# A fused transformer block: a new order of the first weight loads, and matmuls of zeros ahead of the first product

## The chip, the cores and the metric

The kernel runs on one core of a Trainium2 chip. The core has a matrix engine (TensorE, in the profile PE, with its weight loads as PEld), a vector engine (VectorE, DVE), a scalar engine (ScalarE, ACT), a general engine (GpSimd, POOL) and a queue engine (SyncE, SP) that here only issues DMA transfers. The metric is the device time of one execution in microseconds, as the median of several executions; lower is better.

## The reference

The input `x` has 32 sequences of 64 tokens with 1024 features, in float32. The block computes

```
x = x + attention(cond(x, label))
x = x + ffn(cond2(x, language))
```

- `cond(x)` is `x @ W.T` plus a low-rank term whose A factor is picked per sequence by its label (rank 32, 5 labels).
- `attention` projects the result to queries, keys and values (`qkv = c @ w_qkv.T + b_qkv`, 32 heads of 32, 8 key/value heads), applies a rotary embedding, does causal softmax attention within each sequence, and projects back with `w_o`.
- `cond2(x)` is `x @ W.T` plus a mixture of 8 experts of rank 16, the two best of a router with a language bias; `ffn` is the same form with a base matrix, a bias and another router.

Between `cond` and the projection to q, k and v there is no nonlinearity. So the two weight matrices can be multiplied with each other once, and the product applied to the tokens. The same holds for `cond2` and `ffn`.

## The kernel before, in words

All matrices are kept with the contracted dimension on the 128 partitions; 1024 features are 8 chunks of 128 (`KC = 8`, `H = KC // 2 = 4`).

**The stages.** First the kernel multiplies weight matrices: `cq` (the conditioning matrix by the query part of `w_qkv`, 1024 columns), `ckv` (by the key and value part, 512 columns) and `cf` (the second conditioning matrix by the ffn's). The products go to scratch memory in HBM. Then, for each half of the tokens, come the products `qk`, `v`, the attention, `o` and the ffn `f`.

**How one product is done.** A product runs in four groups. A group covers 256 output rows (two blocks of 128), all 8 contracted chunks and two halves of 512 columns. With the two halves of each dimension it is a 2x2 by 2x2 block product, done with seven block products instead of eight (Strassen's method in Winograd's form). Each block product is four matmuls, one per chunk of a half (`mult`, L247 to L259), with 128x512 operands. POOL forms the sums of weight blocks (`weight_sums`, L163 to L174, four operations a group), DVE forms the sums of column blocks (`column_sums`, L176 to L188). In the class `Group` the steps are named p1 to p7:

- `p1` uses the first half of the weights' chunks, left output block (`w[:, :h, :P]`), and chunks 0 to 3 of the columns, left half.
- `p2` uses the second half of the weights' chunks and chunks 4 to 7 of the columns, left half, and adds to p1's bank.
- `p6`, `p5`, `p7` and `p4` use the sums of columns t2, t1, t3 and t4; `p6`, `p5`, `p7` and `p3` use the sums of weights.

**The first product, around which the change lies** (L561 to L638). `wq` holds the columns: 8 chunks of 1024 columns, 512 KB each. `w0` and `w1` are the weights of groups 0 and 1, 1 MB each; the first half of their chunks (`first_half`, 0 to 3) and the second half are loaded apart. `b1` is the other factor of the low-rank term. All these loads are issued by SP, in the written order. The loads before are, in this order: w0's first half, left outputs (256 KB); chunk 0 of wq, left half (256 KB); w0's first half, right outputs; chunk 0, right half; b1 (128 KB); chunks 1, 2, 3 whole (512 KB each); w1's first half; w0's second half; chunks 4 to 7; w1's second half; then `index` and the constants.

**The order on the engines.** Up to L697 SP, TensorE and DVE run in the written order (`manual_schedule`). ACT and POOL are ordered by a planner that estimates when each operation's inputs are ready; behind L697 it orders all engines, except where the code writes an order out again. Loads use eight completion counters in turn, so SP issues a load only when the one eight places before it has landed. TensorE's written order at the start is: p1 of group 0; the first half of `b1q_rows` (b1 by chunks 0 to 3 of wq, both column halves, left first; 16 records of 32 output columns); p1 of group 1; p2 of group 0; the second half of `b1q_rows` (chunks 4 to 7); p2 of group 1; p6 of group 0; and so on (L624, L625, and the dictionary `after`). DVE forms t1 (chunk by chunk, from chunks 0 to 3, right minus left), then t2 (which needs chunks 4 to 7, right halves), then t3; t4 comes after p6 of group 0, with `labels_and_languages`, which needs `index` and the constants.

**Temporaries.** `tmp` (L95) takes one of 11 buffers of 128x512 in SBUF, `ps_tile` (L89) one of 5 banks of PSUM.

Of the kernel before, what the change touches and what calls it, by code (L numbers as in the profile page):

```python
# [19 lines left out]
P = 128  # L20
D = 1024
KC = D // P
# [54 lines left out]
def block_kernel(ctx: ExitStack, tc: tile.TileContext, a, out: bass.AP):  # L77
    nc = tc.nc
# [10 lines left out]
    def ps_tile(name):  # L89
        return psum.tile([P, 512], F32, tag="ps", name=name)  # L90
# [4 lines left out]
    def tmp(name):  # L95
        return tp.tile([P, 512], F32, tag="t", name=name)
# [15 lines left out]
    def load_x(hf):  # L112
# [10 lines left out]
            engines={mybir.EngineType.SP, mybir.EngineType.PE, mybir.EngineType.DVE}  # L123
        )
    )
    bqk, bo, bb = biases[:, 0:10], biases[:, 10 : 10 + KC], biases[:, 10 + KC :]

    lab = const.tile([P, B], F32, tag="lab", name="lab")
# [29 lines left out]
    H = KC // 2  # L158
# [314 lines left out]
    with tc.tile_pool(name="gen", bufs=1) as gen:  # L473
# [87 lines left out]
        wq = gen.tile([P, KC, D], F32, tag="right", name="wq")  # L561
# [3 lines left out]
        b1 = gen.tile([P, KC, LR], F32, tag="b1", name="b1")  # L565
        w0, w1 = (wp.tile([P, KC, WG], F32, tag="w", name=f"w_cq{g}") for g in range(2))
        first_half, second_half = slice(0, H), slice(H, KC)

        for r in range(2):
            cols, outs = slice(r * D // 2, (r + 1) * D // 2), slice(r * P, (r + 1) * P)  # L570
            nc.sync.dma_start(w0[:, first_half, outs], a["w1"][0, :, first_half, outs])
            nc.sync.dma_start(wq[:, 0, cols], a["wqkv"][:, 0, cols])
        nc.sync.dma_start(b1, a["b1"])
        for half in (first_half, second_half):
            for kc in range(max(half.start, 1), half.stop):
                nc.sync.dma_start(wq[:, kc, :], a["wqkv"][:, kc, :D])
            nc.sync.dma_start(w1[:, half], a["w1"][1, :, half])
            if half is first_half:
                nc.sync.dma_start(w0[:, second_half], a["w1"][0, :, second_half])
        nc.sync.dma_start(index, a["index"])  # L580
        nc.sync.dma_start(cst, a["consts"])
        b1q_rows = rank_rows("b1q", b1, wq, D, b1q)
# [188 lines left out]
    for hf in range(2):  # L771
# [396 lines left out]
        for c in range(2):  # L1168
            rows = ps_tile(f"lgrows_{hf}_{c}")
            for kc in range(KC):  # L1170
# [5 lines left out]
                    start=(kc < 4),  # L1176
                    stop=(kc >= 4),
# [3 lines left out]
            for i in range(4):  # L1181
# [5 lines left out]
                    start=True,  # L1187
                    stop=True,
# [63 lines left out]
        ps = ps_tile(f"lgx_{hf}")  # L1252
        for t in range(NT):
# [4 lines left out]
                start=True,  # L1258
                stop=True,
            )  # L1260
        gates3 = gates_of("3", hf, ps[:, : NT * E].rearrange("p (t e) -> p t e", e=E), lg3)
        for c in range(2):
            ps = ps_tile(f"hx_{hf}_{c}")
# [98 lines left out]
```

## Time and profile before

| | |
|---|---|
| time, median of 3 runs | 1222.43 us (1219.89 to 1223.11) |
| the profiled execution's own time | 1215.41 us |
| its span, first to last instruction | 1213.6 us |
| PE busy | 1200.8 us |
| DVE busy | 577.8 us |
| POOL busy | 511.1 us |
| ACT busy | 153.7 us |
| read from HBM, written to it | 83.72 MB, 24.22 MB |

A line of the timeline gives the start in microseconds from the span's start, the length, the engine, the line of the code, the operation, the output and the inputs by name, the shapes and the number of records merged; in brackets stands how long the engine was idle before it and what ended that. A float32 matmul leaves two records. In the list of waits the numbers behind the colon are the total in microseconds, how often, and the longest. In the table of windows each row is a stretch of time, with the busy time of each engine, the clock, the busy share of the DMA engines and the GB/s that they moved.

### The profile page before, as it was taken

Reading aid. Unit: us, or ns where it says so; the run is one execution under the profiler, and the core shown is the slowest. Engines: PE = TensorE matmul, PEld = TensorE weight load, DVE = VectorE, ACT = ScalarE, POOL = GpSimd, SP = SyncE. Lnnn points to the kernel's source line nnn. Section 1 sums busy time; section 2 is a strip of 40 time slices with the busy share of each in tenths; the row PEclk is TensorE's granted clock in tenths of the full one; section 3 lists DMA queues with packets and bytes.
Section 4 is the critical chain, followed back from the end, with each engine's and each line's share of the span. In section 5 each row is a group of like instructions: output and inputs, shape, how many; then the busy total and the mean of one; then the engine's idle time right before and its main releaser. Section 6 shows DMA issues by size and latency. Waiting matters only on the chain.

```text
span 1213.6 us, 13600 instructions
## 1 busy us (share of the span) xinstructions
PE 1200.8 (99%) x5434; PEld 611.3 (50%) x5434; DVE 577.8 (48%) x940; ACT 153.7 (13%) x282; POOL 511.1 (42%) x437
## 2 busy tenths in 40 slices
PE   7999999999999999999999999999999999999998
PEld 2444874555444477544444444444468544444443
DVE  4313151114457789753942113456789764842111
ACT  1000100000001124330000000100214330000000
POOL 4441351442533746754726011542756653821010
PEclk9999999999999999999999999999999999999999
DMA  6562741645111122023114225111120123112110
GB/s 240 186 236 86 263 161 55 205 163 166 35 35 35 36 70 70 12 75 126 36 35 139 69 96 182 36 35 35 35 71 21 51 70 113 63 35 69 56 50 35
DMA packets 58560, 108.83 MB, mean 90 GB/s; under 512 B 5120, under 2 KB 35200, under 8 KB 57216
## 3 DMA queue, kind: packets, MB, share of 16 engines
q1 hardware_dynamic: 42704, 79.53, 19.6%
q10 hardware_dynamic: 13104, 20.03, 4.5%
q0 software_dynamic: 2688, 8.39, 2.1%
q8 instruction: 43, 0.70, 0.2%
q14 instruction: 21, 0.17, 0.0%
HBM read 83.72 MB, written 24.22 MB: 89 GB/s over the span
## 4 chain that ended last, share of the span: by engine, by line
PE 99%; DMA 0%; SPq 0%; DVE 0%; issue 0%; DVEq 0%
PE qk_y L249 9%; PE o_y L249 7%; PE f_y L249 7%; PE qk_x L249 6%; PE qk_z L249 6%; PE v L864 5%; PE f_z L249 5%; PE o_x L249 5%; PE o_z L249 5%; PE f_x L249 5%; PE cq_y L249 3%; PE cf_y L249 3%; PE sc L885 3%; PE cq_x L249 2%; PE pt L938 2%; PE cf_z L249 2%
## 5 line engine op out<-in xcount | busy, mean ns | idle before, releaser
L814 POOL TENSOR_TENSOR raw<-raw,consts 128x512 f32<-128x512 f32 x40 | 63.1, 1586 | 105.8 <-DVE t L813 105.8
L918 POOL TENSOR_TENSOR e<-e,top 128x512 f32<-128x512 f32 x64 | 65.0, 1044 | 57.3 <-DVE top L917 42.2
L930 POOL TENSOR_TENSOR e<-e,tot 128x512 f32<-128x512 f32 x64 | 66.2, 1066 | 27.3 <-DVE tot L928 27.3
L249 PE MATMUL qk_y<-sum_x,s_qk 128*128 128x512 f32 x160 | 72.2, 594 | 0.0
L249 PE MATMUL qk_x<-x,w_qk 128*128 128x512 f32 x160 | 72.2, 594 | 0.0
L170 POOL TENSOR_TENSOR s_f<-w_f 128x512 f32<-128x512 f32 x8 | 11.5, 1437 | 121.2 <-DMA w_f<-cffn 97.4
L249 PE MATMUL o_x<-q,w_o 128*128 128x512 f32 x128 | 58.9, 592 | 0.0
L864 PE MATMUL v<-w_v,x 128*128 128x256 f32 x256 | 58.7, 382 | 0.0
L249 PE MATMUL f_x<-x,w_f 128*128 128x512 f32 x128 | 57.9, 592 | 0.0
L249 PE MATMUL f_y<-sum_y,s_f 128*128 128x512 f32 x128 | 57.5, 592 | 0.0
L1039 POOL TENSOR_TENSOR x<-x,o_u 128x512 f32<-128x512 f32 x24 | 30.9, 1291 | 54.3 <-DVE o_u L1037 33.2
L864 PEld LDWEIGHTS v<-w_v,x 128*128 128x128 f32 x256 | 47.4, 190 | 8.4 <-issue 2.7
L249 PEld LDWEIGHTS qk_x<-x,w_qk 128*128 128x128 f32 x160 | 30.1, 190 | 38.0 <-issue 37.9
L815 DVE TENSOR_TENSOR t<-t,consts 128x512 f32<-128x512 f32 x40 | 48.8, 1231 | 0.7
L249 PEld LDWEIGHTS qk_y<-sum_x,s_qk 128*128 128x128 f32 x160 | 30.2, 190 | 37.1 <-issue 36.6
L170 POOL TENSOR_TENSOR s_qk<-w_qk 128x512 f32<-128x512 f32 x10 | 19.2, 1923 | 65.9 <-DMA w_qk<-cqkv 65.8
L927 DVE TENSOR_REDUCE tot<-e 128x8 f32<-128x512 f32 x64 | 40.5, 667 | 10.7 <-ACT e L922 10.4
L922 ACT ACTIVATE e<-e 128x512 f32<-128x512 f32 x64 | 38.3, 641 | 54.3 <-POOL e L918 54.2
L908 DVE TENSOR_TENSOR e<-sc,consts 128x512 f32<-128x512 f32 x64 | 39.7, 677 | 8.8 <-PE sc L885 8.8
L249 PEld LDWEIGHTS f_x<-x,w_f 128*128 128x128 f32 x128 | 24.3, 190 | 30.6 <-issue 30.6
L249 PEld LDWEIGHTS f_y<-sum_y,s_f 128*128 128x128 f32 x128 | 24.3, 190 | 30.6 <-issue 30.6
L917 DVE TENSOR_REDUCE top<-e 128x8 f32<-128x512 f32 x64 | 39.6, 676 | 0.0
(318 smaller groups left out, 2202.4 us busy)
## 6 DMA issues: line engine op xcount, KB each, us to landing
w_qk<-cqkv SPq DMA_DIRECT2D x10, 1024.0 KB, 6.2
x<-in_xT SPq DMA_DIRECT2D x16, 512.0 KB, 7.7
w_o<-in_wo SPq DMA_DIRECT2D x16, 512.0 KB, 5.2
s_o<-wos SPq DMA_DIRECT2D x16, 512.0 KB, 6.3
w_f<-cffn SPq DMA_DIRECT2D x8, 1024.0 KB, 5.3
outT<-o ACTq DMA_DIRECT2D x32, 256.0 KB, 2.5
cqkv<-cq ACTq DMA_DIRECT2D x16, 256.0 KB, 2.2
w_ckv<-in_w SPq DMA_DIRECT2D x4, 1024.0 KB, 7.2
```

What stands on the lines that cost most here:

```text
L249: nc.tensor.matmul(ps, self.weights[left][:, kc, :], self.right(right, kc), start=first and kc == 0, stop=kc == self.h - 1, skip_group_che ...
L814: nc.gpsimd.tensor_mul(rv, rv, c3)
L815: nc.vector.tensor_mul(t2v, t2v, s3)
L864: nc.tensor.matmul(begun[t], x[kc][:, t * P : (t + 1) * P], wv[:, kc, :], start=False, stop=kc == KC - 1, skip_group_check=True,)
L885: nc.tensor.matmul(sc[j][:, n * S : (n + 1) * S], q[rows, g, b, 2 * mp : 2 * mp + 2, :].rearrange("p m t -> p (m t)"), k[rows, g, b, :], s ...
L908: nc.vector.tensor_add(per_key(e), per_key(sc[j]), mask.unsqueeze(1).to_broadcast([P, 8, S]))
L917: nc.vector.tensor_reduce(top, ev, AX.X, ALU.max)
L918: nc.gpsimd.tensor_sub(ev, ev, wide(top))
L922: nc.scalar.activation(e, e, AF.Exp, scale=SCALE)
L927: nc.vector.tensor_reduce(tot[:, i], es[i], AX.X, ALU.add)
L930: nc.gpsimd.tensor_mul(es[i], es[i], wide(tot[:, i]))
L1039: nc.gpsimd.tensor_add(xo, xo, to)
```

## The change

Two things change. At the start of the written order, DVE sets a temporary of 128x512 to zero, and TensorE multiplies this temporary by itself three times, with 512, 512 and 128 columns, into a bank of PSUM that nobody reads.

The order and cut of the first loads is another. The new order is: w0's first half, left outputs; the left halves of chunks 0 to 3 of wq (four loads of 256 KB); b1; the right halves of chunks 0 to 3; w1's first half; w0's first half, right outputs; w0's second half; chunks 4 to 7; w1's second half. The bytes are the same; three loads more are issued (18 before `index` instead of 15). The order of TensorE's and DVE's other work is as it was.

```diff
@@ -123,6 +123,12 @@
             engines={mybir.EngineType.SP, mybir.EngineType.PE, mybir.EngineType.DVE}
         )
     )
+
+    idle = tmp("idle")
+    nc.vector.memset(idle, 0.0)
+    ps = ps_tile("idle")
+    for n in (512, 512, 128):
+        nc.tensor.matmul(ps[:, :n], idle[:, :P], idle[:, :n], start=True, stop=True)
     bqk, bo, bb = biases[:, 0:10], biases[:, 10 : 10 + KC], biases[:, 10 + KC :]
@@ -566,17 +572,20 @@
         w0, w1 = (wp.tile([P, KC, WG], F32, tag="w", name=f"w_cq{g}") for g in range(2))
         first_half, second_half = slice(0, H), slice(H, KC)
 
-        for r in range(2):
-            cols, outs = slice(r * D // 2, (r + 1) * D // 2), slice(r * P, (r + 1) * P)
-            nc.sync.dma_start(w0[:, first_half, outs], a["w1"][0, :, first_half, outs])
-            nc.sync.dma_start(wq[:, 0, cols], a["wqkv"][:, 0, cols])
-        nc.sync.dma_start(b1, a["b1"])
-        for half in (first_half, second_half):
-            for kc in range(max(half.start, 1), half.stop):
-                nc.sync.dma_start(wq[:, kc, :], a["wqkv"][:, kc, :D])
-            nc.sync.dma_start(w1[:, half], a["w1"][1, :, half])
-            if half is first_half:
-                nc.sync.dma_start(w0[:, second_half], a["w1"][0, :, second_half])
+        outs = [slice(r * P, (r + 1) * P) for r in range(2)]
+        nc.sync.dma_start(w0[:, first_half, outs[0]], a["w1"][0, :, first_half, outs[0]])
+        for c in range(2):
+            cols = slice(c * D // 2, (c + 1) * D // 2)
+            for kc in range(H):
+                nc.sync.dma_start(wq[:, kc, cols], a["wqkv"][:, kc, cols])
+            if c == 0:
+                nc.sync.dma_start(b1, a["b1"])
+        nc.sync.dma_start(w1[:, first_half], a["w1"][1, :, first_half])
+        nc.sync.dma_start(w0[:, first_half, outs[1]], a["w1"][0, :, first_half, outs[1]])
+        nc.sync.dma_start(w0[:, second_half], a["w1"][0, :, second_half])
+        for kc in range(H, KC):
+            nc.sync.dma_start(wq[:, kc, :], a["wqkv"][:, kc, :D])
+        nc.sync.dma_start(w1[:, second_half], a["w1"][1, :, second_half])
         nc.sync.dma_start(index, a["index"])
         nc.sync.dma_start(cst, a["consts"])
         b1q_rows = rank_rows("b1q", b1, wq, D, b1q)
```

## The prediction

> **What bounds the kernel now.** The page comes first: one engine is busy for the whole span, so time can only be won where that engine stands or crawls.
>
> ```profile
> span 1213.6 us, 13600 instructions
> PE 1200.8 (99%) x5434; PEld 611.3 (50%) x5434; DVE 577.8 (48%) x940; ACT 153.7 (13%) x282; POOL 511.1 (42%) x437
> ```
>
> TensorE lacks 12.8 us of the span. The waits of TensorE say where:
>
> ```profile
> PE cq_x L249 <- DMA wq<-in_wqkv: 7.1, 2, 4.7
> PE cq_y L249 <- DVE cq_u L291: 0.8, 1, 0.8
> PE f_z L249 <- issue: 0.6, 1, 0.6
> ```
>
> 7.1 us of it wait for the first weights, in the stretch that the change rewrites; all other waits together are under 2 us. The timeline of TensorE shows the head (start, length, what, records; a 512-column float32 matmul leaves two records):
>
> ```profile
> 4.67 2.05 PE L249 MATMUL cq_x<-wq,w_cq 128*128 128x512 f32 x2 [4.67 <-DMA wq<-in_wqkv]
> 9.15 4.78 PE L249 MATMUL cq_x<-wq,w_cq 128*128 128x512 f32 x6 [2.44 <-DMA wq<-in_wqkv]
> 13.87 1.92 PE L503 MATMUL b1q<-wq,b 128*32 128x512 f32 x16
> 15.72 7.13 PE L249 MATMUL cq_x<-wq,w_cq 128*128 128x512 f32 x16
> 22.78 1.92 PE L503 MATMUL b1q<-wq,b 128*32 128x512 f32 x16
> 24.64 3.70 PE L249 MATMUL cq_x<-wq,w_cq 128*128 128x512 f32 x8
> 28.18 3.60 PE L249 MATMUL cq_y<-sum_cq,s_cq 128*128 128x512 f32 x8
> ```
>
> In program order these are step p1 of group 0 (chunks kc 0 to 3, left halves), the first half of the b1q rows, p1 of group 1 together with p2 of group 0 (chunks 4 to 7), the second half of b1q, p2 of group 1, p6 of group 0. From 13.87 on nothing stands; before it, p1 of group 0 takes from 4.67 to 13.9. Two causes: chunk 1 is there only at 9.15, and the matmuls are slow. The weight loads show the second:
>
> ```profile
> 11.87 0.33 PEld L249 LDWEIGHTS cq_x<-wq,w_cq 128*128 128x128 f32 x1 [0.52 <-DMA wq<-in_wqkv]
> 12.73 0.33 PEld L249 LDWEIGHTS cq_x<-wq,w_cq 128*128 128x128 f32 x1 [0.52 <-issue]
> 17.11 0.19 PEld L249 LDWEIGHTS cq_x<-wq,w_cq 128*128 128x128 f32 x1 [0.24 <-issue]
> 17.54 0.19 PEld L249 LDWEIGHTS cq_x<-wq,w_cq 128*128 128x128 f32 x1 [0.24 <-issue]
> ```
>
> One record each 0.86 us at 12 us, each 0.43 us at 17 us: TensorE runs at half speed until about 13 us. (The clock column reads 1.00 there too; the spacing is the better witness.) Last, when loads land, by who stopped waiting for them:
>
> ```profile
> 6.73 1.15 DVE L182 TENSOR_TENSOR sum_cq<-wq 128x512 f32<-128x512 f32 x1 [6.73 <-DMA wq<-in_wqkv]
> 9.13 0.69 DVE L182 TENSOR_TENSOR sum_cq<-wq 128x512 f32<-128x512 f32 x1 [1.25 <-DMA wq<-in_wqkv]
> 14.33 1.28 POOL L170 TENSOR_TENSOR s_cq<-w_cq 128x512 f32<-128x512 f32 x1 [6.99 <-DMA w_cq<-in_w]
> 15.64 5.70 DVE L184 TENSOR_TENSOR sum_cq<-wq,sum_cq 128x512 f32<-128x512 f32 x4 [3.23 <-DMA wq<-in_wqkv]
> 20.76 1.70 POOL L170 TENSOR_TENSOR s_cq<-w_cq 128x512 f32<-128x512 f32 x1 [0.57 <-DMA w_cq<-in_w]
> ```
>
> Chunk 0 is whole at 6.73, chunk 1 at 9.13 (chunks 2 and 3 at 10.43 and 11.72, by the next two DVE rows), w0's second half at 14.33, chunk 4 at 15.64, w1's second half at 20.76. From 9.13 a 512 KB load lands each 1.28 to 1.30 us, so chunk 7 landed at about 15.64 + 3 x 1.28 = 19.5. The windows say that this stream is full:
>
> ```profile
> 5.00:9.00 4.00, 1.72 (x2) 0.14 (x1) 1.15 (x1) 0.00 (x0) 1.26 (x1) 1.00 0.98 315
> 16.00:20.00 4.00, 4.00 (x10) 1.73 (x10) 4.00 (x3) 0.54 (x1) 3.92 (x3) 1.00 1.03 406
> ```
>
> (The last two columns: DMA share, GB/s.) The DMA engines have no idle time from 5 to 20 us. So there are two bounds in a row: p1 holds TensorE back until 13.9, while the stream, in the same bytes, lets p2 of group 0 end no earlier than chunk 7's landing plus one chunk's two records, 19.5 + 0.86 = 20.4. It ended at 22.78. The gap of 2.4 us is what a faster p1 can win at most with this stream.
>
> **The change part by part.**
>
> *Zeros.* A DVE memset of 128x512 and matmuls of 512, 512 and 128 columns. No DVE memset is in the trace: 0.10 us (POOL's 128x1 memsets) to 1.15 us (the longest L182); I take 0.69, the usual L182 of that size. Engines start at 0.75, so the zeros start at about 1.5. At the slow spacing they are 0.99 (4.67 to 5.66, the first pair) + 3 x 0.86 + 2 x 0.21 for the short one = 4.0 us, to 5.5 (4.9 to 6.0 by the memset's ends). Behind them queues p1, which started at 4.67: 0.8 us later. In exchange it can run at 0.43 a record: before, the spacing fell about 4 us after TensorE resumed at 9.15, and the zeros run for 4. p1 then ends at 5.5 + 8 x 0.43 = 8.9; if zeros do not count for the clock, 4 us after 5.5 it does: 5.5 + 4.0 (4.7 records) + 3.3 x 0.43 = 10.9. Both ends are covered by the next wait.
>
> *Order of loads.* Ahead of p1's last chunk now lie 256 KB of w0 and four pieces of 256 KB (1.3 MB) instead of 2.75 MB. The 1.05 MB ahead of chunk 0's right half landed at 6.73, so 1.3 MB lands at about 7.7 even at the 278 GB/s below, in time for p1's chunk 3 at 5.5 + 6 x 0.43 = 8.1.
>
> *Price of the smaller pieces.* Rows of 2 KB instead of 4 KB for chunks 1 to 3. By the packet records a 2 KB packet took about 87 ns and a 4 KB one 160: eight packets per DMA engine and piece, 2 x 8 x 87 = 1.39 us a chunk against 1.28, so 0.33 us for three chunks. Ends: 0 (nothing lost) and 0.65, if all 1.57 MB move at the 278 GB/s of the first 1.18 MB (to about 6.0) and not in the 5.0 us from 6.73 to 11.72. I take 0.33, which is the same packet at the same place. SP issues three loads more, 0.43 to 0.50 us each; it is ahead of the stream by up to eight loads, so they are hidden. Without that cover: 1.5 us on the stream.
>
> *What the stream gives then.* w0's right outputs (512 packets of 512 B, 32 per engine at 28 ns = 0.9 us) go behind w1's first half. Chunk 3's right half: 11.72 - 0.9 + 0.33 = 11.15. w1's first half was one 1.30 us step after chunk 3, 13.0; now 13.0 - 0.9 + 0.33 = 12.4. From w0's second half on, the bytes ahead are the same: chunk 4 at 15.97, chunk 7 at 19.8, w1's second half at 21.1.
>
> *TensorE then.* b1q's first half waits for the right halves and ends at about 12. p1 of group 1: 12.4 to 15.85. p2 of group 0 is fed by chunks at 15.97, 17.25, 18.5, 19.8: ends 19.8 + 0.86 = 20.7 against 22.78. Then 1.85 of b1q to 22.5 (w1 there since 21.1), p2 of group 1 to 26.0, p6 at 26.0 instead of 28.18. **Gain 2.1 us** (1.75 with 0.65, 2.4 with 0).
>
> *What else moves.* p6 at 26.0 needs DVE's t2 and POOL's second sum. DVE's t2 began at 15.64 and took 5.70; 0.33 later it ends at 21.7. DVE's next four take 5.71, to 27.4, before p6's result at 29.5. POOL's L172 of group 0 ran at 6.08; its input now lands near 13.3. Its reader p7 comes at about 34.5, and POOL's eight sums, 1.27 to 1.72 each, fit between. The second sum ended at 18.5. If that cover were gone, p6 would wait and everything behind it. index and consts go behind three more issues and land near 22, while the consts are first read at 31.6 (29.5 now) and index at 34.9 (32.8). The zeros' bank and temporary are free long before their next use. Later loads wait for TensorE's releases (47.30 and on), so they move with it. The 2.1 us therefore stays to the end, unless the order of the rest changes.
>
> *Sum.* The profiled execution was 1215.41 (span 1213.6 plus 1.8 outside); 1213.3 after. It lay 7.0 under the median of the runs, 1222.43, to which I apply the same difference: **1220.3**.
>
> **Two rules against the rows.** The row: half speed up to 12.73, full at 15.7, in one execution. The Trainium skill (TensorE: Matmul & The Clock Gate, Part 1) says that the clock is halved until a free-running window of about 3.4 us has been busy. By that, an estimate, other executions of before get full speed anywhere from 12.6 to 16.0, b1q would be slow in some, and the gain would be 2.1 to 3.3 us; no run here shows that spread. The other speaks against the change: DMA: Bandwidth & Descriptors (Bandwidth) wants 1 MiB or more per transfer for three quarters of the peak. The trace has 512 KB loads at 406 GB/s because many are under way. If the eight 256 KB pieces ran at half of that, an estimate from the rule, they would cost 5 us more and the kernel would take about 1225.
>
> **The rivals.**
> (A) The stream bounds, as above: 1220.3, own range 1218.8 to 1222.
> (B) The stream gets faster. It carried 315 GB/s at 5 to 9 us against 406 later, 0.9 us worth; were that gone, chunk 7 lands near 18.9 and p2 ends at 19.8: gain 3.0. Past 3.7 us (0.3%, about what a measurement of this kernel tells from no change) it goes only if the typical run of before also loses more at the head than this profile: b1q's 1.85 at half speed is up to 1.85 more, 4.85 in all: 1217.6. For it: the gap of 7 us between profile and median is unexplained. Against: nothing shows where it lies.
> (C) No gain. It needs chunk 7 at 21.9, so chunk 3's right half at 13.25. The data begin at about 1.75 and reach their waiters some 0.65 after the last packet (packet records), so the first 2.49 MB would have to move in 10.85 us, at 229 GB/s, instead of 8.75, at 285. The slowest single microsecond between 2 and 10 us had 248. Time 1222.4.
> (D) Slower: the small pieces starve the stream. Over 0.3% it decides from chunk 7 at 25.6, that is 171 GB/s for the first 2.49 MB. At 165, the mean of 0 to 5 us with its start included, it is 0.6 us beyond: 14.55 becomes 15.1 us, 1226.7. For it: twice as many small packets; against: the same 248.
> (E) The planner reorders ACT, POOL and the later stages after other due times and opens waits there. All waits after the head are under 2 us now; it takes 5.8 us of new ones to be slower by 0.3%, 1226.1. Seven waits as long as the 0.84 us one. Against: all it sees is a shift.
>
> **How the numbers follow.** A 0.60, B over the bound 0.20, C 0.08, D 0.05, E 0.07. Faster by over 0.3%: B, 0.20. Within: A and C, 0.68. Slower: D and E, 0.12. Range 1217.0 to 1225.5: it takes in A, C, most of B (0.05 left below) and leaves D and E above.
>
> **What would show it.** Zeros on TensorE from about 1.5 to 5.5, p1 at 0.43 a record and ended by 9; a short wait at b1q's right half, near 9.9 to 11; w1 near 12.4; p2 with small gaps at each chunk and ended near 20.7; p6 near 26.0; a span near 1211.5. TensorE's waits for wq come back in other places. I am wrong if p6 starts under 24.5 or over 27.5, or if waits for DVE or POOL appear later.

## The result and the profile after

The changed kernel takes 1219.95 us (median of 22 runs), the kernel before 1221.91 us in the same sets of runs (also 22). The ratio is 0.9983, 95% interval 0.9974 to 0.9993: about 2.0 us faster (0.9 to 3.2), inside the 0.3% that was called a tie. The forecast was 1220.3, 2.1 us faster. So the size was right, as closely as an interval that wide can tell. The profile shows that most steps were, that two of them can't be checked as finely as they were worked out, and that one thing had been missed.

The page of the changed kernel:

```profile
span 1216.5 us, 13619 instructions
PE 1204.8 (99%) x5440; PEld 612.9 (50%) x5440; DVE 582.2 (48%) x941; ACT 153.6 (13%) x282; POOL 509.6 (42%) x437
```

This profiled execution is longer than the one of before (1213.6), although the medians go the other way. The timeline of TensorE shows the head (in this file the helper that multiplies is at L255, the zeros at L131, the b1q rows at L509):

```profile
1.47 4.21 PE L131 MATMUL idle<-idle 128*128 128x512 f32 x6 [1.47 <-DVE idle L128]
5.47 4.17 PE L255 MATMUL cq_x<-wq,w_cq 128*128 128x512 f32 x8
9.57 1.92 PE L509 MATMUL b1q<-wq,b 128*32 128x512 f32 x16
11.45 6.07 PE L255 MATMUL cq_x<-wq,w_cq 128*128 128x512 f32 x12
17.70 1.13 PE L255 MATMUL cq_x<-wq,w_cq 128*128 128x512 f32 x2 [0.17 <-DMA wq<-in_wqkv]
18.98 1.12 PE L255 MATMUL cq_x<-wq,w_cq 128*128 128x512 f32 x2 [0.16 <-DMA wq<-in_wqkv]
20.04 1.92 PE L509 MATMUL b1q<-wq,b 128*32 128x512 f32 x16
21.89 3.70 PE L255 MATMUL cq_x<-wq,w_cq 128*128 128x512 f32 x8
25.43 3.60 PE L255 MATMUL cq_y<-sum_cq,s_cq 128*128 128x512 f32 x8
```

The reader sees the forecast order of limits. p1 of group 0 ends near 9.6 instead of 13.9. Then p2 of group 0 is broken into pieces: chunk 6 is awaited until 17.70 and chunk 7 until 18.98. It ends at 20.0 instead of 22.8, and p6 starts at 25.43 instead of 28.18. So 2.75 us are won at the head; the 4.3 us by which p1 of group 0 ends earlier are partly given back to the loads.

Two more views of the head. The whole timeline has the weight loads, whose spacing is TensorE's speed, and those who waited for loads:

```profile
6.32 0.34 PEld L255 LDWEIGHTS cq_x<-wq,w_cq 128*128 128x128 f32 x1 [0.52 <-issue]
6.91 0.19 PEld L255 LDWEIGHTS cq_x<-wq,w_cq 128*128 128x128 f32 x1 [0.25 <-issue]
7.34 0.19 PEld L255 LDWEIGHTS cq_x<-wq,w_cq 128*128 128x128 f32 x1 [0.24 <-issue]
8.10 2.67 DVE L188 TENSOR_TENSOR sum_cq<-wq 128x512 f32<-128x512 f32 x4 [6.69 <-DMA wq<-in_wqkv]
...
15.17 5.45 DVE L190 TENSOR_TENSOR sum_cq<-wq,sum_cq 128x512 f32<-128x512 f32 x4 [4.39 <-DMA wq<-in_wqkv]
...
20.32 1.44 POOL L176 TENSOR_TENSOR s_cq<-w_cq 128x512 f32<-128x512 f32 x1 [0.85 <-DMA w_cq<-in_w]
```

Full speed is there at about 6.6 us; it came at about 13 us before. Chunk 4 landed at 15.17 (15.64 before), w1's second half at 20.32 (20.76 before). The windows (last two columns: DMA share and GB/s) show the stream a little ahead:

```profile
5.00:9.00 4.00, 4.00 (x10) 2.05 (x9) 0.90 (x2) 0.00 (x0) 0.00 (x0) 1.00 1.02 364
16.00:20.00 4.00, 3.58 (x7) 0.89 (x6) 4.00 (x4) 0.00 (x0) 3.39 (x3) 1.00 1.03 405
```

From 5 to 9 us, where the changed kernel loads rows of 2 KB, it moved 364 GB/s; before, with most of these bytes in rows of 4 KB, it moved 315.

Where then did the 2.75 us go? The waits of TensorE:

```profile
PE f_z L255 <- DVE o L1237: 3.0, 1, 3.0
PE idle L131 <- DVE idle L128: 1.5, 1, 1.5
PE f_z L270 <- DVE hwr L774: 1.2, 1, 1.2
PE cq_y L255 <- DVE cq_u L297: 0.8, 1, 0.8
PE cq_x L255 <- DMA wq<-in_wqkv: 0.3, 2, 0.2
```

The wait for wq is nearly gone, and there are two waits that the first profile did not have. They lie at 650 us, in the ffn of the first half of the tokens. TensorE there, before and after:

```profile
644.86 3.60 PE L249 MATMUL f_y<-sum_y,w_f 128*128 128x512 f32 x8
...
654.42 3.70 PE L249 MATMUL f_z<-x,s_f 128*128 128x512 f32 x8 [0.63 <-issue]
```

```profile
642.13 3.60 PE L255 MATMUL f_y<-sum_y,w_f 128*128 128x512 f32 x8
...
649.50 1.12 PE L270 MATMUL f_z<-hwr,b 128*128 128x512 f32 x2 [1.18 <-DVE hwr L774]
...
655.33 5.29 PE L255 MATMUL f_z<-x,s_f 128*128 128x512 f32 x8 [2.99 <-DVE o L1237]
```

And DVE, which frees the bank that the last of these rows waits for:

```profile
654.52 0.75 DVE L1237 SCALAR_TENSOR_TENSOR o<-f_z,consts,f_u 128x512 f32<-128x512 f32 x1 [3.15 <-remote]
```

At the first of these rows the shift of the head is still whole: 642.13 against 644.86, 2.73 us. Then TensorE stands 1.18 and 2.99 us, and behind the second wait eight records take 5.29 us instead of 3.70: the trace's clock records show half clock for 3.41 us from 655.16. That turns -2.7 into +2.5 within 12 us; the last matmul is 2.5 us later than in the profile of before, and the output behind it makes the remaining 0.3 us of the span's 2.8.

DVE is late at that place, and ACT too, but not of themselves: by the trace's semaphore records the semaphore that they wait for, which only TensorE's matmuls raise, moved at 654.50 and 656.62, and they started 0.02 and 0.08 us later. The matmuls that these steps stand for end at 650.63 and 651.49 by the profile, whose matmul ends are modelled. "remote" means that the view found no instruction whose end fits the step. So what comes late is TensorE's own report that a result is there; the trace doesn't say why. Whether the change does this is a question for the experiments.

### The profile page after: what moved, and what is told of

It is laid out like the page before. It is cut to its first block, busy times and chain, and to the rows that moved or that the text cites. A ratio compares the mean times of both kernels' runs of the same rounds, so it can differ in the third digit from the quotient of the medians.

```text
span 1216.5 us, 13619 instructions
## 1 busy us (share of the span) xinstructions
PE 1204.8 (99%) x5440; PEld 612.9 (50%) x5440; DVE 582.2 (48%) x941; ACT 153.6 (13%) x282; POOL 509.6 (42%) x437
## 4 chain that ended last, share of the span: by engine, by line
PE 97%; DMA 1%; DVE 0%; another core or an unknown queue 0%; SPq 0%; ACT 0%; issue 0%; DVEq 0%; ACTq 0%
PE qk_y L255 9%; PE o_y L255 7%; PE f_y L255 7%; PE qk_x L255 6%; PE qk_z L255 6%; PE v L873 5%; PE f_z L255 5%; PE o_x L255 5%; PE f_x L255 5%; PE o_z L255 5%; PE cq_y L255 3%; PE cf_y L255 3%; PE sc L894 3%; PE pt L947 2%; PE cf_z L255 2%; PE cq_z L255 2%
## 5 line engine op out<-in xcount | busy, mean ns | idle before, releaser
L255 PE MATMUL qk_x<-x,w_qk 128*128 128x512 f32 x160 | 72.2, 594 | 0.0
L255 PE MATMUL qk_y<-sum_x,s_qk 128*128 128x512 f32 x160 | 72.2, 594 | 0.0
L255 PE MATMUL o_x<-q,w_o 128*128 128x512 f32 x128 | 58.9, 592 | 0.0
L255 PE MATMUL f_x<-x,w_f 128*128 128x512 f32 x128 | 57.9, 592 | 0.0
L255 PE MATMUL f_y<-sum_y,s_f 128*128 128x512 f32 x128 | 57.5, 592 | 0.0
L255 PEld LDWEIGHTS qk_x<-x,w_qk 128*128 128x128 f32 x160 | 30.1, 190 | 38.0 <-issue 37.9
L255 PEld LDWEIGHTS qk_y<-sum_x,s_qk 128*128 128x128 f32 x160 | 30.2, 190 | 37.1 <-issue 36.6
L1237 DVE SCALAR_TENSOR_TENSOR o<-f_z,consts,f_u 128x512 f32<-128x512 f32 x16 | 12.0, 751 | 58.6 <-PE f_z L265 42.6
L255 PEld LDWEIGHTS f_y<-sum_y,s_f 128*128 128x128 f32 x128 | 24.3, 190 | 30.6 <-issue 30.6
L255 PEld LDWEIGHTS f_x<-x,w_f 128*128 128x128 f32 x128 | 24.3, 190 | 30.6 <-issue 30.6
```

The costliest lines, as they stand in the source:

```text
L255: nc.tensor.matmul(ps, self.weights[left][:, kc, :], self.right(right, kc), start=first and kc == 0, stop=kc == self.h - 1, skip_group_che ...
```

## The experiments

The theory: the stream of loads bounds p2 of group 0, by chunk 7's landing, and TensorE has time to spare ahead of it. The rivals: full speed, bought by the zeros, makes the gain; or TensorE's own chain bounds the head. The second question is the stall at 650 us. The runs came in three sets, each on another chip; kernels of one set share their runs of before, whose median was 1215.60, 1218.55 and 1215.39 us. So ratios are compared, not times from set to set.

### The loads alone, and the zeros alone

The first takes the zeros out of the changed kernel:

```diff
-    idle = tmp("idle")
-    nc.vector.memset(idle, 0.0)
-    ps = ps_tile("idle")
-    for n in (512, 512, 128):
-        nc.tensor.matmul(ps[:, :n], idle[:, :P], idle[:, :n], start=True, stop=True)
```

> The new loads without the zeros. Stream theory (p2 of group 0 ends when chunk 7 is there, and TensorE has some 1.7 us to spare before): p1 starts near 4.4, is slow until about 8.4, ends near 10; p6 of group 0 starts at 25.4 +- 0.3 as in the changed kernel, and the gain on before stays near 2 us. Rival (the full speed bought by the zeros makes the gain): TensorE stays slow until about 13 as it did before, p6 starts at 27 or later and most of the gain is gone.

Measured: ratio 0.9980 (0.9971 to 0.9989), 2.4 us faster than before. TensorE:

```profile
5.03 6.70 PE L249 MATMUL cq_x<-wq,w_cq 128*128 128x512 f32 x8 [5.03 <-DMA wq<-in_wqkv]
11.65 1.92 PE L503 MATMUL b1q<-wq,b 128*32 128x512 f32 x16
13.51 5.59 PE L249 MATMUL cq_x<-wq,w_cq 128*128 128x512 f32 x12
19.26 1.12 PE L249 MATMUL cq_x<-wq,w_cq 128*128 128x512 f32 x2 [0.16 <-DMA wq<-in_wqkv]
20.56 1.13 PE L249 MATMUL cq_x<-wq,w_cq 128*128 128x512 f32 x2 [0.17 <-DMA wq<-in_wqkv]
...
27.00 3.60 PE L249 MATMUL cq_y<-sum_cq,s_cq 128*128 128x512 f32 x8
```

p1 of group 0 takes 6.7 us at half speed, p1 of group 1 starts 2 us later than in the changed kernel, and yet TensorE still catches up with the stream and waits for chunks 6 and 7. The stream itself was later in this execution (20.56 against 18.98 for chunk 7), so p6 missed the expected 25.4 and fell on the 27 that the rival had named; the time did not. Full speed came at 11.1 us by the clock records, after the 8.4 of the expectation and before the 13 of the rival. The gain of the loads alone is clear of the noise, so the zeros are not what makes it. Whether they add or take a little in this order can't be said: the two kernels were never timed in one set, and the intervals of 0.9980 and 0.9983 leave room for 1 to 2 us either way.

The second puts the same lines of zeros into the kernel before.

> The zeros with the loads of before. Stream theory: p1 is bound by chunks 1 to 3 (9.15, 10.44, 11.73) and, at full speed, ends near 12.6 instead of 13.9; p6 starts near 26.8 instead of 28.18, a gain of 1.35 us, less than the whole change. Rival (the speed falls back while TensorE waits from 6.4 to 9.15 for chunk 1): p1 is slow again, p6 starts at 28.2 and nothing is gained. Second rival (the zeros make the whole gain): p6 near 25.4.

Measured: ratio 0.9999 (0.9990 to 1.0008), nothing gained. The first rival is what happened. TensorE in that kernel:

```profile
9.67 1.12 PE L255 MATMUL cq_x<-wq,w_cq 128*128 128x512 f32 x2 [3.60 <-DMA wq<-in_wqkv]
10.95 3.45 PE L255 MATMUL cq_x<-wq,w_cq 128*128 128x512 f32 x4 [0.16 <-DMA wq<-in_wqkv]
...
28.82 3.60 PE L255 MATMUL cq_y<-sum_cq,s_cq 128*128 128x512 f32 x8
```

And in its windows (the clock is the third value from the right):

```profile
12.00:14.00 2.00, 2.00 (x3) 0.59 (x2) 0.69 (x1) 0.00 (x0) 0.00 (x0) 0.50 1.04 422
```

The zeros had brought full speed by 4.5 us (clock records), chunk 1 came 3.6 us after chunk 0 was used up, and the clock went back to half from 11.32 for 3.41 us. The two parts belong together in one direction only: new loads need no zeros, but zeros are thrown away without new loads.

### More zeros

```diff
-    for n in (512, 512, 128):
+    for n in (512, 512, 128, 512, 512, 512, 512):
```

> The changed kernel with four more 512-column matmuls of zeros, 3.44 us at full speed. Stream theory: p1 ends near 12.5 instead of 9.1, b1q near 14.4, p1 of group 1 near 17.8, p2 near 21.3 without waiting for chunks; p6 starts at 26.5, only 1.1 us later than in the changed kernel, since the rest of the 3.44 us was spent waiting for the stream. Rival (TensorE's own chain bounds the head): all 3.44 us show, p6 at 28.9.

Measured: ratio 0.9991 (0.9982 to 1.0000), 0.9 us faster than before.

```profile
9.78 3.60 PE L255 MATMUL cq_x<-wq,w_cq 128*128 128x512 f32 x8
...
15.16 7.13 PE L255 MATMUL cq_x<-wq,w_cq 128*128 128x512 f32 x16
...
27.62 3.60 PE L255 MATMUL cq_y<-sum_cq,s_cq 128*128 128x512 f32 x8
```

The added zeros cost 4.3 us (9.78 against 5.47), not 3.44, since they ran at half speed until 7.2 us. Of these 4.3 us, 2.2 show at p6 against the changed kernel's first profile, and about 1.4 in the time (0.9 us gained, against 2.3 of the changed kernel in the third set, where before was equally fast). p2 of group 0 has no waits for chunks left: here TensorE's own chain is the bound. Delay ahead of the stream is partly free, as the theory has it; the expected 1.1 was too small mostly because the zeros were 0.9 us longer.

### Left halves of the second four chunks

If chunk 7's landing is the bound, half of it is enough: p2 uses left halves only.

```diff
-        for kc in range(H, KC):
-            nc.sync.dma_start(wq[:, kc, :], a["wqkv"][:, kc, :D])
-        nc.sync.dma_start(w1[:, second_half], a["w1"][1, :, second_half])
+        for c in range(2):
+            cols = slice(c * D // 2, (c + 1) * D // 2)
+            for kc in range(H, KC):
+                nc.sync.dma_start(wq[:, kc, cols], a["wqkv"][:, kc, cols])
+            if c == 0:
+                nc.sync.dma_start(w1[:, second_half], a["w1"][1, :, second_half])
...
-                (0, "p2"): load_first,
+                (1, "p2"): load_first,
```

(`load_first` holds the second half of the b1q rows and the first loads of x. It has to move, as these rows need the right halves; its move alone was not run. The work of TensorE ahead of p6 stays the same.)

> The changed kernel, but chunks 4 to 7 are loaded as left halves first, then w1's second half, then the right halves; and the second half of the b1q rows stands behind p2 of group 1. If chunk 7's landing bounds p2 of group 0, its left half now lands near 16.6 and p2 runs without waits from 14.9 to 18.4, p2 of group 1 to 21.9, b1q to 23.7, and p6 starts near 23.7 instead of 25.4: 1.7 us faster than the changed kernel, near 3.7 us faster than before. If something else bounds the head (DVE's t2, POOL's sums), p6 stays at 25 or later.

Measured: ratio 0.9964 (0.9950 to 0.9978), 4.2 us faster than before. p2 of both groups ran without waits, but w1's first half landed only at 12.87 in the profiled execution, so p6 started at 25.22 and not at 23.7, which by the words of the expectation would speak for another bound. It was therefore run once more in the third set, beside the changed kernel and a version without the zeros.

> Left halves of chunks 4 to 7 ahead of w1's second half and the right halves, b1q's second half behind p2 of group 1, once more. p2 of group 0 without waits for chunks; p6 at 23.8 if w1's first half lands at 11.5, as in the changed kernel's first profile, and each microsecond later with it. If the stream is the bound of the changed kernel, it is 0.5 to 1.7 us faster than the changed kernel on the same chip; if not, equal.

Measured: ratio 0.9964 (0.9952 to 0.9976), 1210.91 us.

```profile
11.66 10.57 PE L255 MATMUL cq_x<-wq,w_cq 128*128 128x512 f32 x24 [0.35 <-DMA w_cq<-in_w]
...
24.01 3.70 PE L255 MATMUL cq_y<-sum_cq,s_cq 128*128 128x512 f32 x8
```

With w1 at 11.66, 24 records run in one piece and p6 starts at 24.01, as expected. The changed kernel in the same set:

> The changed kernel beside the two below, on one chip. p6 of group 0 at 25.4 to 25.7 as in its two profiles; 2 to 3 us faster than before if TensorE does not stall near 650 us, less clear if it does.

Measured: ratio 0.9983 (0.9974 to 0.9992), 1213.09 us, so the left halves are 2.2 us faster than it, more than the expected 0.5 to 1.7.

```profile
12.74 3.70 PE L255 MATMUL cq_x<-wq,w_cq 128*128 128x512 f32 x8 [0.31 <-DMA w_cq<-in_w]
...
20.53 1.12 PE L255 MATMUL cq_x<-wq,w_cq 128*128 128x512 f32 x2 [0.17 <-DMA wq<-in_wqkv]
...
26.98 3.60 PE L255 MATMUL cq_y<-sum_cq,s_cq 128*128 128x512 f32 x8
```

Its chunk 7 landed at 20.53 this time and p6 started at 26.98, outside the expected 25.4 to 25.7: p6 follows chunk 7 by 6.45 us in all its profiles (18.98 to 25.43, 19.17 to 25.61, 20.53 to 26.98), which is the bound once more. This late chunk 7 also makes part of the 2.97 us between the two profiles at p6.

> The same without the zeros: p1 of group 0 runs from about 5.0 at half speed until 8 to 11 and ends at 10 to 11.8; b1q ends at 12 to 13.7. If w1's first half lands at 11.5 to 12.9, p1 of group 1 starts 0 to 2 us later than with the zeros, and p6 with it: the zeros are worth 0 to 2 us in this order, where TensorE is not held back later.

Measured: ratio 0.9971 (0.9961 to 0.9982), 1211.69 us. p1 of group 0 ran from 4.84 to 11.2, mostly at half speed, p1 of group 1 started at 13.07 and p6 at 25.43, 1.4 us behind the version with zeros in this set and 0.2 behind its profile in the first; 0.8 us in the time, with intervals of the two ratios that overlap. Where the stream no longer holds TensorE back behind p1, the zeros seem to be worth something, inside the 0 to 2 us expected.

### All left halves first

The radical form: w0, left 0 to 3, w1's first half, w0's second half, left 4 to 7, w1's second half, then b1, w0's right outputs and the right halves 0 to 7; b1q wholly behind p2 of group 1.

```diff
-                (0, "p1"): lambda w: b1q_rows[0](),
-                (0, "p2"): load_first,
+                (1, "p2"): lambda w: (b1q_rows[0](), load_first(w)),
```

> All left halves first: w0, left 0 to 3, w1's first half, w0's second half, left 4 to 7, w1's second half, then b1, w0's right outputs and all right halves; TensorE does p1 of both groups, p2 of both, and the b1q rows behind them. Stream theory: nothing that TensorE needs early waits behind bytes that it needs late, so it runs from 5.5 on almost without waits: 4 x 3.44 + 2 x 1.85 = 17.5 us, p6 near 23, 2.4 us earlier than in the changed kernel, if DVE's t2 (right halves 4 to 7 near 20) is there by then; near 5 us faster than before. Rival: t2 is late, p6 waits for DVE and starts at 25 or later, no faster than the changed kernel.

Measured: ratio 1.0014 (0.9998 to 1.0030), no gain. From its timeline:

```profile
10.07 10.57 PE L255 MATMUL cq_x<-wq,w_cq 128*128 128x512 f32 x24 [0.50 <-DMA w_cq<-in_w]
...
18.04 6.16 DVE L188 TENSOR_TENSOR sum_cq<-wq 128x512 f32<-128x512 f32 x4 [16.62 <-DMA wq<-in_wqkv]
...
24.12 6.76 DVE L190 TENSOR_TENSOR sum_cq<-wq,sum_cq 128x512 f32<-128x512 f32 x4
...
26.02 1.10 PE L255 MATMUL cq_y<-sum_cq,s_cq 128*128 128x512 f32 x2 [1.70 <-DVE sum_cq L190]
```

The rival won. All four p1 and p2 are done by 20.6, earlier than in any other version, but DVE could start on t1 only at 18.04 (8.10 in the changed kernel), and t1 and t2 take 12.9 us one behind the other, 6.16 and 6.76. In the changed kernel they took 2.67 and 5.45; there t1 ran before POOL's first sum, here POOL's sums run beside all of it. Whether that is what slows DVE was not varied. p6 waits for DVE at each of its four chunks, first until 26.02 and 3.3 us in all. The cover of DVE, which the prediction had named, was spent.

> The same without the zeros. If the zeros were worthless only because the stream bounded the head, they count here, where TensorE's own chain bounds it: p1 starts near 4.8 at half speed until 8.5 to 11, so p6 is 1.3 to 2.5 us later than with the zeros. If the zeros are worth nothing anywhere, the two are equal.

Measured: ratio 1.0013 (0.9997 to 1.0029). p6 starts at 25.12, also after a wait for DVE, and waits for it four times (2.4 us in all): in time equal to the version with zeros, because the new bound is DVE and not TensorE. So this pair can't say what the zeros are worth where TensorE's own chain bounds the head.

### The stall at 650 us

> The changed kernel once more, beside the others. Stream theory: as fast as the new loads alone, 2 to 2.5 us faster than before, p2 of group 0 again fed by chunks. The waits near 650 us (1.2 and 3.0 us of TensorE, and a stretch at half clock behind them) are either chance, then they are not here and the shift of the head reaches the end whole; or the change makes them (its shift brings two things together there), then they are here again.

Measured: ratio 0.9995 (0.9979 to 1.0011), undecided: in this set single runs spread from 1215 to 1225 us, and the medians even stand the other way, 1219.23 against 1218.55 us of before. The expected 2 to 2.5 us are not seen here. p6 started at 25.61; near 650 us TensorE waited once, 2.05 us, and the clock stayed whole:

```profile
653.29 3.70 PE L255 MATMUL f_z<-x,s_f 128*128 128x512 f32 x8 [2.05 <-issue]
```

> The kernel before, a second profile. Where p1 of group 0 ends and where TensorE gets to full speed: if the first 14 us repeat, p6 of group 0 starts at 28.2 +- 0.3; if the stream or the clock varies from execution to execution, p6 differs by a microsecond or more, and heads can only be compared with that much doubt.

Measured: 1220.84 us, with p6 at 28.79 and full speed at 14.2 us instead of 13.1. So heads of single profiles can be compared to 0.6 us at best, and by the three of the changed kernel to 1.5. The waits of TensorE in the kernel before:

```profile
PE cq_x L249 <- DMA wq<-in_wqkv: 7.2, 2, 4.6
PE f_z L249 <- DVE o L1228: 3.0, 1, 3.0
PE f_z L264 <- DVE hwr L765: 1.1, 1, 1.1
```

These are the same two waits, and half clock for 3.41 us follows them (from 659.34). So the change does not make them. All four kernels profiled in the second set had waits of 2.0 to 4.1 us at that place, none of the seven profiled in the first and third had any. The semaphore records say the same: in the seven, TensorE's semaphore moved within 0.02 us of the modelled end of its matmuls there; in the four, and in the first profiles of before and after, it moved up to 5 us late. As each set had its own chip, the stall goes with the chip or with the time of the set, and not with the kernel. Its cause stays open: it was not varied.

## Why the prediction was right

**What bounds the kernel.** Right. Two bounds in a row: p1 of group 0, and behind it the stream. p6 follows chunk 7 by 6.45 us in three executions, and halving what p2 needs of the chunks gave another 2.2 us in the time.

**Zeros.** The sum was right, its parts not quite: DVE started at 0.93 and needed 0.48, not 0.75 and 0.69, and the zeros started at 1.47, near the forecast 1.5. p1 started at 5.47, 4.98 and 5.47 in the three profiles (5.5) and ended at 9.6, 8.6 and 9.9 (8.9, at worst 10.9). That both ends are covered by the next wait fits: without the zeros the loads still gain 2.4 us. So in this order no run shows a gain from the zeros. The working said nothing of what happens to the clock if TensorE waits again; in this order it does not matter, with the loads of before it cancels the zeros.

**Order of loads and price of the pieces.** The forecast was w1 at 12.4, chunk 4 at 15.97 and chunk 7 at 19.8. In three executions w1 was used at 11.45, 11.83 and 12.74, and chunk 7 at 18.98, 19.17 and 20.53. The forecast lies inside, but the term of 0.33 us for 2 KB rows can't be confirmed: the stream varies by 1.5 us from one execution to another. It did not fall to half, as the estimate from the rule on large transfers had it: it moved 364 GB/s. Here that rule of the Trainium skill (DMA: Bandwidth & Descriptors, Bandwidth) does not bind. That this is so because many transfers are under way at once is likely, as a 512 KB load of before landed 8.4 us after its issue while one landed each 1.3 us, but no run varied it.

**TensorE then.** Gain at p6 forecast 2.1. Measured from the first profiles 2.75, from the second 3.18, while the third profile of the changed kernel has p6 at 26.98, a gain of 1.2 to 1.8 against the two of before. By the medians of the timed sets it is 2.0 us faster, 0.7 slower (undecided, 0.6 faster by the ratio) and 2.3 faster. The forecast agrees with the first and the third set; that it came within 0.4 us of the measured time is partly luck. The short wait at b1q's right half, announced between 9.9 and 11, was absent in the first profile and there in the others, whose b1q took 2.79 and 2.65 us instead of 1.92.

**What else moves.** Right as to the head: no new wait for DVE's t2, POOL's sums, the consts or index. But the prediction called itself wrong if waits for DVE appeared later, and in the first profile they did, 1.2 and 3.0 us near 650 us, with a span of 1216.5 and not 1211.5. As the kernel before shows the same waits in its second profile, and the third profile of the changed kernel (span 1211.6) has none, they do not come from the change; the sign did not tell the two apart. When the all-left order spent DVE's cover, it cost all the gain.

**The rivals.** (B), a faster stream, happened in part in one execution and not in another; it never reached 0.3%. (C) and (D), a slower stream, did not happen in any profile: chunk 7 was there at 20.53 at the latest, and (C) needs 21.9. (E), a new order of ACT, POOL and the later stages, did not happen: in the traces of before and after ACT and POOL have the same operations on the same tiles in the same order, and TensorE and DVE differ by the zeros alone.

**What was missed.** The profile of before lay 7 us under the median, and the text left that gap unexplained. A large part of it is very likely the stall near 650 us: up to 4.2 us of waits, and 1.7 us by half clock for 3.41 us, against 0.6 in that profile. The sets whose profiles show the stall have medians of before of 1221.91 and 1218.55 us, the two without it 1215.60 and 1215.39, next to that profile's 1215.41. A forecast of 2 us had to stand beside that, and only because it strikes both kernels could the medians show it.

**The clock.** By the clock records full speed came at 13.1 and 14.2 us in the two profiles of before, 3.9 and 5.0 after TensorE's second start; with zeros at 4.5 to 7.2, which is 3.0 to 5.8 after theirs; in the changed kernel without its zeros at 11.1, 6.1 after its start. Where the clock fell and rose again, it stayed at half for 3.413 us, and the full stretches before that lasted 6.83, 645.12, 648.53 (twice) and 651.95 us: 2, 189, 190 and 191 times 3.413. The Trainium skill (TensorE: Matmul & The Clock Gate, Part 1) says that the clock is set by a window of about 3.4 us that runs freely and does not start with the kernel, and these figures bear it out. It also says that the first 3.4 us or so run at half speed; in two executions it was 3.0, and the measurement decides.

## What to carry to other kernels

When an engine waits at the start, list what each of its steps needs and when these bytes can be there; the gain ends where the next step meets the stream, and here loading less for that step moved it on. Zeros to warm up TensorE can pay only if nothing makes it wait again and its own chain is the bound behind them, and reordering loads for one engine must leave the others their early inputs: the form that fed TensorE best starved DVE and lost the whole gain. A change of 0.2% is read from the shift of one record far behind the change, and from ratios inside one set of runs, not from the span of one profile.

## What the runs showed of the hardware

In these runs TensorE's clock fell to half with short pauses. With waits of 2.98 to 3.60 us it was halved, each time for 3.41 us, from 0.2 us before the end of the wait to 1.7 us after it: in the kernel with zeros alone, in the changed kernel, in the second profile of before and in both all-left kernels; with the single wait of 2.05 us it was not. Matmuls of zeros bring full speed: in two kernels it came at 4.5 and 7.2 us, when TensorE had run nothing else. The stream of first loads varied by 1.5 us for the same program. And near 650 us the semaphore that TensorE's matmuls raise moved within 0.02 us of their modelled ends in seven profiles, and up to 5 us behind them in the first profile of the changed kernel; ACT and DVE started as soon as it moved.
